# Rearranging a three-layer hybrid kernel: one image's linear attention beside the other's convolutions, and expert tiles between written attention steps

## The chip, the cores and the metric

The kernel runs on one core of a Trainium2 chip, as one program. The metric is the device time in microseconds (us). A core has five instruction streams: TensorE (PE, with its weight loads shown apart as PEld), VectorE (DVE), ScalarE (ACT), GpSimd (POOL) and SyncE (SP, which here only issues DMAs).

## The reference, cut to what matters

All arithmetic is fp32. The input is `x` of shape (2, 256, 56, 56): two images, 256 channels, 3136 pixels each.

```python
# layer 0, for each image
x = x + conv_ref(group_norm(x))
#   y = w_qkv1 @ x           1x1 convolution, 256 -> 768 channels
#   y = depthwise 3x3 of y   768 channels
#   q, k, v = y.reshape(B, H, W, 3, 8 heads, 32)     a raw reshape
#   heads 0-3: 7x7 neighbourhood attention; heads 4-7: the same, dilated by 2
#   o = w_proj @ heads
# layer 1 on t = the 2 x 3136 tokens of 256 features
t = t + attn(layernorm(t))
#   Q, K = elu(x Wq) + 1, elu(x Wk) + 1
#   KV = K^T v, summed over the image; msg = Q KV / (Q . sum K), then Wm, layernorm
#   h = relu([x, msg] W1) W2;  x + layernorm(h)
t = t + ffn(layernorm(t))
#   router: 8 experts, top 2 of softmax(x Wr + br)
#   each expert: layernorm, 256 -> 1024, gelu, 1024 -> 256; weighted sum of the two
```

The sum KV runs over a whole image, so no token's linear attention can start before the keys of all tokens of its image have been summed. The reshape mixes channels with pixels, so the attention of layer 0 can start on its first rows when the first channel groups are convolved.

## The kernel before, in words

The work is cut by image and by kind.

*Convolutions* (`convolutions`, L511). Each image has six groups of 128 output channels (`oc`), each in two halves of 28 rows: 12 blocks for an image. A block does the 1x1 convolution on TensorE (`py`, L531: four row groups) with a copy by ScalarE into a padded buffer (`ypad`, L537; there are two of them, one for each half). The 3x3 convolution is shared between the engines: eight of the 28 rows are nine matmuls with diagonal weights (`pc`, L552; GpSimd makes the diagonals at L520), the other 20 rows are one ScalarE and eight VectorE instructions (`yc`, L565 and L570). The block is stored to DRAM (`yd`).

*Neighbourhood attention* (`attend`, L736 and on). An image has 44 chunks: 28 of `band0` (not dilated) and 16 of `band1` (dilated). A chunk is: scores for four heads (L602, into `s_ps`, the only buffer of its kind, four PSUM banks), one exponential (L606), one multiplication by a table of biases and masks on VectorE (L607), then the values and the denominators (L612, into `po`, two banks), which VectorE adds to strips (L619). Queries and keys come by transposes of loaded rows (`prepare`, L685, through `s_ps` too). Finished strips are normalised (L629 to L639) and projected (`project`, L362 and L367), and the tokens go to DRAM (`td`).

*Linear attention* (`layer1`). For each pair of 128-token tiles, `keys` (L272) takes statistics, transposes, multiplies by Wk, applies elu and adds to `kx`. Then groups of four tiles go through four functions: `queries` (L1656 to L1670), `message` (L1696), `feed_forward` (L1726, L1742) and `route` (L1807 and on), which also scatters each token's row to its experts' lists in DRAM (`xs`, POOL queue, L161). Each function yields at its steps, and strings such as `"mqfpPPPPcufmuqfurfvrfvfv"` write out the order of these steps, one letter for each.

*Experts* (`Experts.run`). A tile is up to 256 rows of one expert: `fetch` loads the rows and 2.1 MB of weights, `turn` transposes, 32 matmul instructions make the hidden layer, with eight gelus (L1407, L1411), then 16 for each half of the rows make the output (L1425), and a scatter adds the rows to `y2`. A tile has eight steps. There are 48 full tiles and five half ones.

The order of the work: image 1's convolutions; from its third channel group on, image 1's attention beside them; image 2's convolutions beside the rest of that; then image 2's attention beside the keys of image 1 (`first_keys`); then all of the linear attention, the keys of image 2 within its first six steps. Four expert tiles (`NFI = 4`) lie between the last steps of the linear attention, the others come after it. In the first part a planner sets the order on each engine, from written priorities and estimated costs: each convolution step is followed by `PACE = 2` attention steps. From `layer1` on, TensorE's instructions run in the written order (`manual_schedule`); the other engines' orders are the planner's throughout. SP issues nearly all DMAs, in one queue that runs in order.

```python
for k, (b, blocks_done) in enumerate(convolutions()):       # front
    ...
    advance(PACE)
...
for k, _ in enumerate(first_keys(tokens, ps_e)):
    advance(3)
advance(10**6)
```

A pool's memory is used again by the next stage's pools. `NE1 = 32` is the number of token tiles after whose routing the first table of expert tiles is made.

Of the kernel before, what the change touches and what calls it, by code (L numbers as in the profile page):

```python
# [27 lines left out]
NA = -(-T // 128)  # L28
NH = 4
# [5 lines left out]
PACE = 2  # L35

# [16 lines left out]
NE1, NE2 = 32, 36  # L53
# [5 lines left out]
NFI = 4  # L59
# [60 lines left out]
def hybrid_kernel(ctx: ExitStack, tc: tile.TileContext, a: dict, out: bass.AP):  # L120
# [64 lines left out]
    class Tokens:  # L185


        def __init__(self, run):
            self.run = run
            self.rt, self.xa, self.kw = ExitStack(), ExitStack(), ExitStack()  # L190
            rt = self.rt.enter_context(tc.tile_pool(name=f"rt{run}", bufs=1, side="right"))

            self.t_ab = rt.tile([P, 1, C], F32, name="t_ab")
            self.xT_ab = rt.tile([P, 2, P], F32, name="xT_ab")

            self.up = rt.tile([P, NF], F32, name="up_t")
            self.cnt = rt.tile([P, E], F32, name="cnt")
            nc.gpsimd.memset(self.cnt, 0.0)

            xa = self.xa.enter_context(tc.tile_pool(name=f"ta{run}", bufs=1, side="right"))  # L200
            self.image = xa.tile([P, (NA + 1) * C], F32, name="t_a")
            self.t = [self.image[:, : (NA - 1) * C].rearrange("p (n c) -> p n c", c=C), None]

        def open(self):

            run = self.run
            xa = self.xa.enter_context(tc.tile_pool(name=f"xa{run}", bufs=1, side="right"))
            self.xT = [xa.tile([P, 2, (NA - 1) * P], F32, name="xT_a"), None]

            self.shared = self.image[:, (NA - 1) * C :].rearrange("p (n c) -> p n c", c=C)  # L210

            self.kxs = xa.tile([P, 2, C], F32, name="kxs0")
            self.kc = xa.tile([P, 2], F32, name="kc0")
            self.w_k = xa.tile([P, 2, C], F32, name="w_k")
            nc.gpsimd.dma_start(self.w_k, a["L1_attn_Wk"].rearrange("(k p) o -> p k o", p=P))
            self.b2 = xa.tile([P, C], F32, name="b2")
            nc.gpsimd.dma_start(self.b2, a["L1_attn_b2"].partition_broadcast(P))
            self.one = xa.tile([P, 1], F32, name="one")
            nc.vector.memset(self.one, 1.0)

        def at(self, n0, n):
# [3 lines left out]
            if n0 < NA:  # L225
                return self.t[0][:, n0 : n0 + n, :]
            k = (n0 - NA) % 4
            return self.t[1][(n0 - NA) // 4][:, k : k + n, :]

        def turned(self, n0, n):  # L230
# [4 lines left out]
            return self.xT[h][:, :, (n0 - h * NA) * P : (n0 - h * NA + n) * P]  # L235

        def load(self, n0, n, eng=nc.sync):
            self.loaded = eng.dma_start(
                self.at(n0, n), td[n0 * P : (n0 + n) * P, :].rearrange("(n p) c -> p n c", p=P)
            ).ins  # L240

    def elu1(wk, dst, src, tag, bufs):

        m = wk.tile([P, 512], F32, name=f"elu_{tag}", tag="tmp", bufs=bufs)[:, : src.shape[1]]
# [4 lines left out]
    def stats(sm, t, deviation=None):  # L249

        n = t.shape[1]
        st = sm.tile([P, max(n, 2), 6], F32, name="st")
        mv = sm.tile([P, 4, 2], F32, name="mv")
# [3 lines left out]
        return mv, rstd(sm, mv[:, :n, 1], 1.0, deviation)  # L257

    def rstd(sm, var, scale, deviation=None):
        n = var.shape[1]  # L260
        r = sm.tile([P, 2, 4], F32, name="rs")
        with tc.high_priority():
            nc.vector.tensor_scalar(r[:, 1, :n], var, scale, 1e-5, ALU.mult, ALU.add)  # L263
            newest[1] = nc.gpsimd.tensor_tensor(r[:, 0, :n], r[:, 1, :n], mhalf[:, :n], ALU.pow).ins  # L264
# [4 lines left out]
    def keys(tk, wk, sm, ps, bufs, kx, acc, n0, n):  # L269


        t = tk.at(n0, n)  # L272
        mv, rs = stats(sm, t, tk.up[:, n0 : n0 + n])
        xt = wk.tile([P, 2, C], F32, name="xt")
# [1825 lines left out]
```

## Time and profile before

| | |
|---|---|
| Median of three runs | 2033.22 us (2032.94 to 2037.04) |
| The profiled execution's own time | 2033.13 us |
| Its span, first to last instruction | 2031.3 us |
| Mean granted TensorE clock | 0.970 of full speed |
| Busy | PE 1871.8 us, PEld 1322.6, DVE 1034.5, ACT 617.3, POOL 654.5 |
| DMA | 264.65 MB, mean 130 GB/s |

The span is cut at these places, read from the timeline: at 437 us the last projection of image 1 has run and the first transposes of image 2's attention begin; from 757 us the queries of the linear attention run; at 840 us its steps are in rhythm; from 1162 us expert weights are loaded; at 1340 us the fifth expert tile starts, with nothing but experts after it. A busy share below the highest is not idle time by itself: the question in each stretch is which engine's work has to be waited for.

### The profile page before, as it was taken

What the parts mean: (1) busy time and instruction counts of PE and PEld (TensorE: products, weight loads), DVE (VectorE), ACT (ScalarE), POOL (GpSimd) and SP (SyncE); (2) the same over time, 40 slices, a digit from 0 to 9 for tenths busy, and PEclk for the clock granted to TensorE, in tenths of its full rate; (3) what the DMA queues carried; (4) which work ended last, traced back from release to release, by engine and by line L of the source; (5) the groups of instructions that cost most, each with busy time, mean ns of one, the idle gap of its engine ahead of it and who ended that gap; (6) DMA issues with size and microseconds to landing.
All of it is one profiled execution on the core that took longest, in us unless ns stands there. A gap on an engine that the chain in (4) does not pass through costs nothing.

```text
span 2031.3 us, 27712 instructions
## 1 busy us (share of the span) xinstructions
PE 1871.8 (92%) x10050; PEld 1322.6 (65%) x10050; DVE 1034.5 (51%) x2625; ACT 617.3 (30%) x1222; POOL 654.5 (32%) x776
## 2 busy tenths in 40 slices
PE   4999898999787888999999998999999999999995
PEld 2544454554445455665665657888888888888885
DVE  4987987877875666456555654442112211111221
ACT  1333334323232232333333323322222222222332
POOL 4522100122034234335434344523333332333321
PEclk9999899999889799999999999999999999999998
DMA  5542423344422125000111143577676767666995
GB/s 117 141 112 73 154 86 97 101 134 117 127 64 68 33 55 170 5 16 32 53 42 55 43 151 102 175 194 212 194 197 187 197 191 204 189 199 192 290 284 158
DMA packets 189976, 264.65 MB, mean 130 GB/s; under 512 B 26488, under 2 KB 149702, under 8 KB 189584
## 3 DMA queue, kind: packets, MB, share of 16 engines
q1 hardware_dynamic: 160912, 220.82, 35.4%
q0 software_dynamic: 20640, 29.76, 7.7%
q10 hardware_dynamic: 8272, 12.15, 1.7%
q8 instruction: 83, 1.36, 0.3%
q14 instruction: 69, 0.57, 0.1%
HBM read 196.39 MB, written 70.55 MB: 131 GB/s over the span
## 4 chain that ended last, share of the span: by engine, by line
PE 75%; DVE 10%; DMA 5%; POOL 3%; issue 3%; ACT 3%; SPq 0%; ACTq 0%; DVEq 0%; POOLq 0%
PE ph L1407 16%; PE py L1425 16%; PE p L1726 7%; PE pc L552 6%; PE py L531 5%; PE po L612 5%; PE py L1742 4%; PE s_ps L367 2%; PE kx L310 2%; DVE yc L570 2%; PE s_ps L602 2%; DMA y<-yt,idi 2%; PE kp L297 2%; DVE p L607 2%; PE pm L1696 2%
## 5 line engine op out<-in xcount | busy, mean ns | idle before, releaser
L1407 PE MATMUL ph<-xe,w1e 128*128 128x256 f32 (+1 forms) x1696 | 362.4, 371 | 3.2 <-DVE xe L1383 2.1
L1425 PE MATMUL py<-w2e,hT 128*128 128x256 f32 x1616 | 359.1, 379 | 0.0
L1411 ACT ACTIVATE hT<-ph,sv 128x256 f32<-128x256 f32 (+1 forms) x424 | 196.1, 463 | 498.9 <-PE ph L1407 496.1
L1407 PEld LDWEIGHTS ph<-xe,w1e 128*128 128x128 f32 x1696 | 310.2, 191 | 45.4 <-DVE xe L1383 3.0
L1425 PEld LDWEIGHTS py<-w2e,hT 128*128 128x128 f32 x1616 | 302.4, 190 | 39.0 <-issue 0.2
L570 DVE SCALAR_TENSOR_TENSOR yc<-ypad,w,yc 128x1120 f32<-128x1120 f32 x192 | 266.3, 1388 | 33.6 <-ACT yc L565 30.2
L161 POOL DMA_INDIRECT y<-yt,idi x101 | 160.7, 1591 | 218.9 <-DVE yt L1431 127.0
L552 PE MATMUL pc<-ypad,diag 128*128 128x448 f32 x432 | 177.5, 549 | 1.6 <-POOL acc L465 1.6
L1363 DVE CAST idi<-xr 128x2 int32<-128x2 f32 (+1 forms) x53 | 9.3, 176 | 317.2 <-DMA xr<-xs 306.5
L531 PE MATMUL py<-t_a,wq 128*128 128x448 f32 (+1 forms) x384 | 149.4, 525 | 11.4 <-DVE t_a L506 11.0
L1431 DVE SCALAR_TENSOR_TENSOR yt<-py,eq,yt 128x256 f32<-128x256 f32 x101 | 48.7, 483 | 207.6 <-PE py L1425 207.6
L606 ACT ACTIVATE p<-s_ps 112x952 f32<-112x952 f32 (+5 forms) x88 | 102.0, 1159 | 152.8 <-PE po L612 84.3
L264 POOL TENSOR_TENSOR rs<-rs,mhalf 128x2 f32<-128x2 f32 (+2 forms) x89 | 66.0, 749 | 239.9 <-DVE rs L263 188.1
L607 DVE TENSOR_TENSOR p<-p,tab 112x952 f32<-112x952 f32 (+5 forms) x88 | 125.1, 1425 | 32.1 <-ACT p L606 32.0
L520 POOL TENSOR_SCALAR diag<-ident,w 128x128 f32<-128x128 f32 x108 | 87.8, 831 | 142.8 <-PE pc L552 125.4
L552 PEld LDWEIGHTS pc<-ypad,diag 128*128 128x128 f32 x432 | 79.9, 192 | 70.4 <-issue 64.1
L531 PEld LDWEIGHTS py<-t_a,wq 128*128 128x128 f32 x384 | 70.2, 193 | 75.8 <-issue 58.8
L161 POOL DMA_INDIRECT xs<-row,si x98 | 99.1, 1011 | 63.3 <-DVE si L1862 30.1
L1389 POOL TENSOR_SCALAR yt<-b2e,eq 128x256 f32<-128x256 f32 x101 | 47.1, 473 | 224.2 <-DMA b2e<-in_L_ffn_b 217.8
L612 PE MATMUL po<-p,v 98*32 98x170 f32 (+5 forms) x960 | 77.8, 380 | 39.5 <-DVE p L607 16.7
L1742 PE MATMUL py<-fw,hTl 128*128 128x264 f32 x392 | 91.4, 389 | 3.3 <-DVE u L1749 3.3
L1726 PE MATMUL p<-m2T,fw 128*128 128x512 f32 (+2 forms) x224 | 94.1, 543 | 0.0
(388 smaller groups left out, 2522.7 us busy)
## 6 DMA issues: line engine op xcount, KB each, us to landing
w1e<-in_L_ffn_W SPq DMA_DIRECT2D x53, 1024.0 KB
w2e<-in_L_ffn_W SPq DMA_DIRECT2D x53, 1024.0 KB
yd<-yc SPq DMA_DIRECT2D x24, 784.0 KB
ld<-yd SPq DMA_DIRECT2D x28, 448.0 KB
xr<-xs SPq DMA_DIRECT2D x48, 260.0 KB
b2e<-in_L_ffn_b SPq DMA_DIRECT2D x53, 128.0 KB
yr<-y SPq DMA_DIRECT2D x11, 512.0 KB
td<-t_i SPq DMA_DIRECT2D x24, 224.0 KB
```

What stands on the lines that cost most here:

```text
L161: ins = nc.gpsimd.indirect_dma_start(out=dst[:, :], out_offset=bass.IndirectOffsetOnAxis(ap=index, axis=0), in_=src, in_offset=None, **kw,)
L531: nc.tensor.matmul(py[:, :n, :], wq1[:, ct, oc * P : (oc + 1) * P], x_sb[:, ct, (q0 + g0) * WW : (q0 + g0 + n) * WW], start=(ct == 0), sto ...
L552: nc.tensor.matmul(pc, diag[:, tap, :], ypad[:, dy : dy + 8, dx : dx + WW], start=(tap == 0), stop=(tap == 8),)
L570: nc.vector.scalar_tensor_tensor(yc[:, 8:, :], src, w, yc[:, 8:, :], ALU.mult, ALU.add)
L606: nc.scalar.activation(p[:nk, :, :n], s_ps[:nk, :, :n], AF.Exp)
L607: nc.vector.tensor_tensor(grid(p), grid(p), table[:nk], ALU.mult)
L612: nc.tensor.matmul(dst[hs] if w is None else den[hs], v[:nk, hs] if w is None else w[:nk, :], grid(p)[:, h, :, o : o + q.shape[2]], start= ...
L1407: nc.tensor.matmul(p1, x.w1[:, ct, j * P : (j + 1) * P], x.xe[:, ct, :], start=(ct == 0), stop=(ct == 1),)
L1411: nc.scalar.activation(hT[:, j, :], p1, AF.Gelu, bias=x.sv[:, 4 + j : 5 + j])
L1425: nc.tensor.matmul(py, hT[:, j, h * P : (h + 1) * P], x.w2[:, j, :], start=(j == 0), stop=(j == NJ - 1),)
L1726: nc.tensor.matmul(p1[:, :w], fw1[:, k, oc * P : (oc + 1) * P], rhs, start=(k == 0), stop=(k == 3))
L1742: nc.tensor.matmul(py[:, : C + E], hT[:, kk, c0 : c0 + P], fw2[:, kk, :], start=(kk == 0), stop=(kk == 3),)
```

## The change

- **Classes.** `front` is taken apart into a class `Convolutions`, a class `Attention` (one object for each image) and `first_image`.
- **First image.** `first_image` runs the convolutions of image 1 as before, and image 1's attention beside them with two steps for each convolution step, three once image 2's convolutions have begun. When that attention has ended, `conv.share`'s pools are closed, and `run` (the rest of the convolutions) is handed on. By the counts of the two generators this happens in the fourth of image 2's 12 blocks; before, with two steps throughout, it happened in the sixth.
- **Convolutions alone.** The eight blocks that are left use no diagonals and no `pc` matmuls: all 28 rows are done by ScalarE (first tap) and VectorE (eight taps), in two strips of 14 rows. Each of these blocks has nine steps. They have one PSUM bank.
- **Linear attention by image.** `linear(ph, tk, half)` makes pools, loads and functions for one image, so all weights are loaded and prepared twice (`feed`, `router`). The first image's keys and six groups (24 tiles) run in written TensorE order, with a convolution step for each `k` in the strings and two for each key pair. Its summed keys (`sums[0]`) are stashed in DRAM for the tile that both images share. All loads are on SP; before, most weights were on POOL's queue. `keys` loses the code for a shared tile: each image takes its half of tile 24 itself.
- **Fills.** The 16 stores of constant rows into `y2` and `xs` (4.3 MB) were issued at the second step of the linear attention; now they are issued behind the first image's last scatter and ahead of the second image's attention.
- **Second image's attention.** It runs alone in written TensorE order. Scores of a chunk come before the values of the chunk before it (`pending`); transposes and projections are single pieces (`side`) that stand at the places between them; at places that have no such piece, an expert tile's step is issued: after all scores, and after values when the step's number is a multiple of four. They have two PSUM banks together. The first 12 places make the table of expert tiles.
- **Then** the second image's keys and groups, with expert steps at `e` and two for each key pair. `NFI` is 13 in place of 4, `NE1` 24 in place of 32, and `hT`, the hidden layer's tile, has one buffer in place of two.

The core of the diff, with the parts that were only moved left out:

```diff
-NE1, NE2 = 32, 36
+NE1, NE2 = 24, 36
...
-NFI = 4
+NFI = 13
+LEAD = 12
...
+        def alone(self):
+            self.dp, self.banks = None, self.banks[:1]
...
                 for hf in range(2):
+                    shared = SHARE if self.dp is not None else 0
...
+                    strips = [(SHARE, HH // 2)] if shared else [(0, HH // 4), (HH // 4, HH // 2)]
                     for tap in range(9):
...
+                        for y0, y1 in strips:
...
-                        if tap % 3 == 2:
+                        if tap % 3 == 2 if shared else tap % 2 == 0:
                             yield b, oc
...
+            def side():
+                if turning:
+                    turning.popleft()[1]()
+                elif aside and aside[0][0] <= count[0]:
+                    aside.popleft()[1]()
+                else:
+                    return False
+                return True
+            def step(first, rest, then, n=1):
...
+                first()
+                yield "aside" if side() else "scores"
+                if pending:
+                    for f in pending.popleft():
+                        f()
+                pending.append((rest, then))
+                count[0] += 1
+                yield "aside" if side() else "values"
...
+            for _ in range(PACE + b):
+                if need is not None and need <= done:
+                    need = next(steps, None)
+            if need is None:
+                break
+        ctx.close()
+        return run
...
-                hT = self.w.tile([P, NJ, ST], F32, name="hT")[:, :, : nh * P]
+                hT = self.w.tile([P, NJ, ST], F32, name="hT", bufs=1)[:, :, : nh * P]
...
+            ln = linear(ph, tk, 0, behind)
+            with tc.manual_schedule(engines={mybir.EngineType.PE}):
+                for i, _ in enumerate(ln.keys()):
+                    if i == 5:
+                        ln.feed()
+                    if i % 3 != 1:
+                        fill()
+                fill(2)
+                merging = ln.close()
+                prepared = ln.router()
+                parts = (
+                    "qkwkxkwkxkwkxkqk", "mkqkmkqk", "mkqkfkmqfkfkfkffk",
+                    "mqfkfkPPPPmqfrfkrffk", "mqfkpPPPPfkmqfrfrkff", "mqfkpPPPPfkmqfrfrkff",
+                    "mkfkpPPPPfkmfrfrkff", "fkpPPPPkfkfrfkrfkf", "kpPPPPkrkkrkk", "kpPPPPk",
+                )
...
+                ln.keep()
+                nc.sync.dma_start(y2[N : N + ST, :], a["c_fill"][0, :, 0:C])
+                for i in range(NDUM):
+                    rows_i = slice(E * RG + i * ST, E * RG + (i + 1) * ST)
+                    nc.sync.dma_start(xs[rows_i, :], a["c_fill"][E + i])
...
+                att = Attention(ph, 1, "l t b k v p r x ac", bank)
+                with tc.manual_schedule(engines={mybir.EngineType.PE}):
+                    for i, what in enumerate(att.run()):
+                        if i < LEAD:
+                            next(table, None)
+                        elif what == "scores" or what == "values" and i % 4 == 0:
+                            next(tiles, None)
...
+                for i, _ in enumerate(ln.keys()):
+                    if i == 5:
+                        ln.feed()
+                    if i % 3 != 1:
+                        next(tiles, None)
...
+                parts = (
+                    "qewexewexewexeqe", "meqemeqe", "meqefemqfefefeff",
+                    "mqfpPPPPfmqfrfrff", "mqfpPPPPfmqfrfrff", "mqfpPPPPfmqfrfrff",
+                    "mqfpcfmfqrfPPfPrPfe", "mqfpfmfqePePrePfePref", "mfefpefmeferePPfePerPe",
+                    "fefeepefeferePfePere", "eeeeperPePer", "eeeepP",
+                )
```

## The prediction

> **What bounds the kernel now.** I read the page's engine totals and slices first, then busy times by stretch, then groups by line, then what TensorE waited for in the weakest stretch.
>
> ```profile
> PE 1871.8 (92%) x10050; PEld 1322.6 (65%) x10050; DVE 1034.5 (51%) x2625; ACT 617.3 (30%) x1222; POOL 654.5 (32%) x776
> PE   4999898999787888999999998999999999999995
> DVE  4987987877875666456555654442112211111221
> PEclk9999899999889799999999999999999999999998
> ```
>
> TensorE bounds the whole, but its bad slices are the eleventh to sixteenth, where no engine is full and the clock is low. The stretches (columns: length; busy PE, PEld, DVE, ACT, POOL with counts; clock; DMA):
>
> ```profile
> 0.00:255.00 255.00, 213.93 (x1100) 110.30 (x1104) 200.86 (x228) 75.44 (x118) 88.40 (x114) 0.97 0.45 119
> 255.00:437.00 182.00, 172.19 (x1280) 93.04 (x1269) 153.45 (x171) 61.02 (x79) 27.07 (x39) 0.99 0.34 97
> 437.00:550.00 113.00, 102.43 (x636) 54.04 (x635) 86.96 (x116) 35.94 (x56) 15.35 (x18) 0.95 0.46 122
> 550.00:757.00 207.00, 164.98 (x1439) 100.41 (x1438) 127.17 (x240) 63.60 (x82) 67.78 (x83) 0.88 0.23 65
> 757.00:840.00 83.00, 72.54 (x318) 51.11 (x317) 49.76 (x137) 24.99 (x57) 39.55 (x59) 0.96 0.34 104
> 840.00:1162.00 322.00, 315.13 (x1240) 199.78 (x1239) 189.26 (x776) 109.60 (x290) 129.90 (x148) 1.00 0.12 39
> 1162.00:1340.00 178.00, 163.15 (x768) 125.68 (x767) 88.19 (x490) 57.56 (x136) 80.14 (x93) 0.96 0.46 141
> ```
>
> From the first convolutions to 437, VectorE is the fuller partner (153 of 182 us, 84%). From 550 to 757 (image 2's attention, image 1's keys) PE is 80% busy at clock 0.88 and VectorE 61%: latency, not work. From 840 PE is 98% busy. After 1340 there are only experts. So 437 to 840 has idle time to fill, and the end has work that could fill it.
>
> ```profile
> L1407 PE MATMUL ph<-xe,w1e 128*128 128x256 f32 (+1 forms) x1696 | 362.4, 371 | 3.2 <-DVE xe L1383 2.1
> L1425 PE MATMUL py<-w2e,hT 128*128 128x256 f32 x1616 | 359.1, 379 | 0.0
> L570 DVE SCALAR_TENSOR_TENSOR yc<-ypad,w,yc 128x1120 f32<-128x1120 f32 x192 | 266.3, 1388 | 33.6 <-ACT yc L565 30.2
> L552 PE MATMUL pc<-ypad,diag 128*128 128x448 f32 x432 | 177.5, 549 | 1.6 <-POOL acc L465 1.6
> L606 ACT ACTIVATE p<-s_ps 112x952 f32<-112x952 f32 (+5 forms) x88 | 102.0, 1159 | 152.8 <-PE po L612 84.3
> L607 DVE TENSOR_TENSOR p<-p,tab 112x952 f32<-112x952 f32 (+5 forms) x88 | 125.1, 1425 | 32.1 <-ACT p L606 32.0
> L1411 ACT ACT_TABLE_LOAD x5 | 6.4, 1283 | 8.3 <-PE ph L1407 8.3
> PE po L612 <- DVE p L607: 8.4, 8, 3.8
> ```
>
> One expert tile costs (362.4 + 359.1) / 50.5 = 14.3 us of PE (48 full, 5 half). The last row, from the waits of 437 to 757, shows PE held for a chunk's exponential and table product.
>
> **The change, part by part**, against the profiled span of 2031.3 us.
>
> *Stage 1, to the end of image 1's attention: 414 us.* Before, 437. The third attention step per convolution step ends the same attention two blocks sooner. Two blocks take 16 x 1.388 = 22 us of VectorE, the fuller engine, and 2 x (177.5 + 149.4)/24 = 27 us of PE: I take 23.
>
> *Stage 2, image 1's linear attention beside eight blocks: 360 us.* Removed: 8 x 177.5/24 = 59 us of PE and four sets of diagonals on POOL (36 x 0.83 = 30 us, hidden). Added: VectorE does 28 rows in 16 instructions of 784 elements instead of 8 of 1120. No such form is in the trace; scaling 1388 ns by length gives 0.97 us, unscaled it would be 1.39. I take 0.97, as instructions of 512 elements take 0.68. So 8 x 16 x 0.97 = 124 us of VectorE (to 178). The rest of VectorE: 13 key pairs at about 3.6 us (statistics, norms, copy, elu) = 47; a group, from 840 to 1162, (189.3 - 8 x 3.6)/7.75 = 20.7, six are 124; preparations about 13. Sum 308. PE: routing matmuls (L1853) come 42 us apart while two key pairs are in each step and 33 us apart after, so 33 a group and some 4 a pair; blocks 6.2 (149.4/24): 52 + 196 + 50 + 8 = 306. Both are equally full, in orders fixed beforehand. At VectorE's 84 to 89% of the convolution stretches (start-up of 30 us left out): 346 to 367, I take 356, plus 4 at the start. ScalarE's copies into `ypad` wait for VectorE's taps of two blocks earlier; queued behind them are elu, relu and squares, for which PE waits.
>
> *The hand-over, in stage 3: 20 us.* The fills, hidden before, now wait for the last scatters of image 1 (8 at 1.0 us behind the last routing). On SP, the image-2 loads can queue behind them: 4.3 MB at the 173 to 190 GB/s that loading stretches show is 23 us. If SP is ordered around them it costs 8; if all in series, 40. I take 20, nearest to the fills alone.
>
> *Stage 3, image 2's attention with 4.4 expert tiles: 225 us with the hand-over.* 114 places, 37 of them with an expert step: two start, 35 make 4.4 tiles. VectorE: half of lines 607, 619 and the smaller ones, 135 us, and 14 for the tiles: 149. PE: half the attention rows, 178 (overlapping ones counted twice, so 110 to 178), plus 63: 173 to 241. ScalarE: exponentials 51, copies 15, gelus 16, and table switches. Each hidden-layer step stands between two exponentials: 19 steps, 38 loads of 1.28 us = 49. Sum 131. None is full; 205 is the middle of PE's bounds, against 207 for 550 to 757, which had the keys' 50 us of PE in place of 63 for tiles, and much of the attention done before it.
>
> The Trainium skill ("ScalarE: Activation LUTs", What ACT_TABLE_LOAD costs) speaks against interleaving: it gives about 2.66 us for a switch, with a drain, and advises batching. The trace has the gelu start 1.29 us after the load does. By the page ScalarE would hold 183 us in this stage, still under 205.
>
> *Stage 4, image 2's keys and groups with 8.6 tiles: 416 us.* PE: 52 + 6.25 x 32.5 + 8 + 8.6 x 14.3 = 386. The shares before were 98% (840 to 1162) and 92% (1162 to 1340, with tiles): at 95%, 406. Plus 10: the preparation stands at the sixth key step and needs weights that are loaded behind 3 MB of tokens.
>
> *Stage 5, experts alone: 563 us.* 2031.3 - 1340 = 691.3, less nine tiles at 14.3. One buffer for `hT` costs nothing: PE's order already puts a tile's last output matmul before the next tile's first hidden one. If the cover failed, a gelu of 0.46 us per tile would show, 16 us.
>
> Sum: 414 + 360 + 225 + 416 + 563 = 1978; the run takes 1.8 more than its span: **1980**, 53 under. The profiled run is 0.1 below the median, so no correction.
>
> **The rivals.**
>
> *All seams close*: expert steps fill every gap, the fills hide. Stage 2 at VectorE's 92% is 335, stage 3 is 190, stage 4 is 400: 1904. For: from 840 on, written order gave PE 98%. Against: never with convolutions beside it.
>
> *Slower: VectorE holds up stage 2.* Its 308 us are as long as PE's, so every late tap stops ScalarE, then PE, then VectorE's own next inputs. At the 70% between 550 to 757 (61%) and 437 to 550 (77%) the stage takes 440 and the total is 2060. It decides above 413 us, a share below 75%. Unscaled 784-element taps (1.39) would do it as well: 362 / 0.87 = 416. For: 33.6 us of idle before L570. Against: the earlier convolution stretches kept 84%.
>
> *The hand-over eats it*: fills, weights and row loads in one SP queue stop attention again and again; stage 3 takes 275 and the total is 2030, no change. For: SP alone now issues all. Against: DMA was 23% busy from 550 to 757.
>
> **How the numbers follow.** Forecast 0.52 (its own range 1935 to 2022), all seams close 0.25, VectorE 0.18, hand-over 0.05. Within 0.2%, 4 us, is about what this kernel's runs can tell from no change. Faster: 0.52 + 0.25 less 0.01 of the forecast's tail, 0.76; same 0.04; slower 0.20. The range reaches down to 1910, near the second case, and up to 2045 into the third.
>
> **What would show it.** Right: `pc` (L552's successor) has 288 instructions, not 432; PE busy near 1820; some 60 table loads; from the last expert-only tile count, 35 full tiles in about 500 us; VectorE above 80% beside the late convolutions; a PE gap of 10 to 30 us before image 2's first transposes. Wrong: stage 2 over 400 us, or stage 3 over 260 with PE waiting for row loads, or the expert tiles more than 14.5 us apart.

## The result and the profile after

The changed kernel takes 2175.26 us (median of four runs, 2169.75 to 2191.33) against 2033.39 us for the kernel before on the same chip. The ratio is 1.0708, 95% interval 1.0659 to 1.0756: 142 us slower, where 53 us faster had been forecast. The profiled execution is the longest of the four, 2191.33 us with a span of 2189.5 us, so the stage lengths below hold about 16 us more than a median run. Part of that is in stage 1, where its clock was 0.93 and which took 439 us; the kernels below that leave this stage as it is show 428 to 439.

From the page of the changed kernel, the engine totals and the slices (40 slices of the span, in tenths):

```profile
PE 1878.1 (86%) x9960; PEld 1331.2 (61%) x9960; DVE 1080.8 (49%) x2712; ACT 682.3 (31%) x1275; POOL 631.3 (29%) x729
PE   4999897657889991589977988999969999999996
DVE  4979986476867664256645332554452122121121
PEclk9999898778899995599988999999979999999998
```

Before, the weak slices were the eleventh to the sixteenth. Now weak ones are spread from the seventh to the thirtieth, and one is nearly empty (the sixteenth: PE at 1, the clock at 5). PE busy did not fall by the 59 us counted for the removed `pc` matmuls; it rose by 6. The matmuls that stayed took longer: the mean granted clock fell from 0.970 to 0.928, and a hidden-layer matmul between attention steps took 414 ns on average, where 371 ns is the average before. The 54 that came on top, most of them for the weights' second preparation, are few.

```profile
L1514 PE MATMUL x<-xe,w1e 128*128 128x256 f32 x152 | 41.1, 414 | 2.2 <-ACT hT L1518 1.2 <-DVE kT L181 0.7 <-DVE yt L1538 0.2
```

Busy time by stretch, changed kernel (columns: stretch; length; busy PE, PEld, DVE, ACT, POOL with counts; clock; DMA share; GB/s):

```profile
0.00:439.00 439.00, 364.53 (x2270) 194.09 (x2271) 323.85 (x374) 126.27 (x179) 94.25 (x124) 0.93 0.37 101
446.00:566.00 120.00, 86.40 (x321) 63.09 (x320) 91.03 (x177) 29.70 (x51) 68.20 (x75) 0.84 0.16 50
566.00:701.00 135.00, 121.83 (x395) 71.17 (x396) 94.51 (x215) 48.14 (x117) 14.05 (x15) 0.91 0.08 29
701.00:845.00 144.00, 118.02 (x463) 70.99 (x462) 101.31 (x384) 38.79 (x99) 64.07 (x61) 0.92 0.22 72
845.00:884.00 39.00, 8.42 (x39) 5.99 (x42) 6.57 (x40) 2.84 (x7) 12.94 (x17) 0.50 0.53 152
884.00:1144.00 260.00, 217.85 (x1988) 139.16 (x1984) 137.19 (x233) 121.72 (x145) 29.97 (x37) 0.88 0.51 135
1151.00:1279.00 128.00, 109.56 (x494) 90.41 (x495) 50.94 (x164) 46.66 (x72) 70.28 (x92) 0.93 0.38 110
1279.00:1419.00 140.00, 129.40 (x508) 85.11 (x508) 56.43 (x190) 53.32 (x122) 22.98 (x27) 1.00 0.17 49
1419.00:1613.00 194.00, 166.89 (x761) 122.58 (x760) 95.34 (x505) 54.85 (x142) 83.84 (x90) 0.93 0.28 82
1613.00:2189.00 576.00, 553.77 (x2730) 488.03 (x2730) 118.29 (x411) 160.03 (x344) 168.44 (x186) 0.98 0.73 213
```

Row by row: image 1's attention ends; image 1's keys; its ramp, from the first queries to the first routing; the rest of its groups; the hand-over; image 2's attention with tiles; image 2's keys; its ramp; the rest with tiles; experts alone. Two seams of 7 us, ahead of each key stretch, are left out. The two key stretches take 120 and 128 us. In the kernel before there was no such stretch at all. From 446 to 845 VectorE is 72% busy (286.9 of 399 us), not over 80%, and TensorE 82% (326 us).

What TensorE waited for from 446 to 845 (the first two lines) and from 845 to 900 (the third), and SP's own queue from 845 to 900 (the fourth); columns: us in total, times, longest:

```profile
PE kx L301 <- DVE ks L238: 32.5, 13, 11.1
PE pp L1953 <- DVE chosen L1945: 19.2, 1, 19.2
PE x L705 <- DMA ld<-yd: 34.5, 6, 24.4
SPq L2073 <- DMA xs<-row,si: 14.2, 1, 14.2
```

The key phase waits for its own elu, once per pair (`ks`). The end of image 1's half waits once for 19 us, behind convolution taps that stand between the small steps of the last routing on VectorE. Then the fills wait on SP for the scatters to land, the row loads of image 2's attention stand behind them, and TensorE waits for those (34.5 us).

Each stage against the prediction, in us of the profiled execution:

| Stage | Predicted | Measured | Over |
|---|---|---|---|
| 1, to the end of image 1's attention | 414 | 439 | 25 |
| 2, image 1's linear attention | 360 | 406 | 46 |
| Hand-over and 3, image 2's attention | 225 | 299 | 74 |
| 4, image 2's keys and groups | 416 | 469 | 53 |
| 5, experts alone | 563 | 576 | 13 |

The overruns add to 211 us, the distance from the predicted sum of 1978 to the span. No one stage carries it.

### The profile page after: what moved, and what is told of

The parts are those of the page before. It is cut to its first block, busy times and chain, and to the rows that moved or that the text cites. A ratio compares the mean times of both kernels' runs of the same rounds, so it can differ in the third digit from the quotient of the medians.

```text
span 2189.5 us, 27684 instructions
## 1 busy us (share of the span) xinstructions
PE 1878.1 (86%) x9960; PEld 1331.2 (61%) x9960; DVE 1080.8 (49%) x2712; ACT 682.3 (31%) x1275; POOL 631.3 (29%) x729
## 4 chain that ended last, share of the span: by engine, by line
PE 63%; DVE 15%; DMA 8%; issue 4%; ACT 4%; POOL 4%; SPq 1%; DVEq 0%; POOLq 0%; ACTq 0%
PE ph L1514 13%; PE py L1532 12%; PE p L1826 7%; DVE yc L545 5%; PE py L506 4%; PE po L614 4%; PE pc L525 4%; PE kx L301 2%; DMA y<-yt,idi 2%; PE s_ps L600 2%; PE py L1842 2%; PE pq L1756 2%; PE pm L1796 2%; PE s_ps L341 1%; POOL rs L255 1%
## 5 line engine op out<-in xcount | busy, mean ns | idle before, releaser
L1514 PE MATMUL ph<-xe,w1e 128*128 128x256 f32 (+1 forms) x1544 | 334.9, 373 | 8.4 <-DMA w1e<-in_L_ffn_W 4.4
L1532 PE MATMUL py<-w2e,hT 128*128 128x256 f32 x1488 | 337.0, 382 | 0.0
L545 DVE SCALAR_TENSOR_TENSOR yc<-ypad,w,yc 128x1120 f32<-128x1120 f32 (+1 forms) x256 | 315.2, 1237 | 26.9 <-ACT yc L540 23.6
L1514 PEld LDWEIGHTS ph<-xe,w1e 128*128 128x128 f32 x1544 | 283.4, 193 | 48.7 <-issue 5.5
L1518 ACT ACTIVATE hT<-ph,sv 128x256 f32<-128x256 f32 (+1 forms) x386 | 177.5, 462 | 428.4 <-PE ph L1514 425.8
L506 PE MATMUL py<-x_sb,wq 128*128 128x448 f32 (+1 forms) x384 | 151.6, 529 | 14.4 <-DVE x_sb L477 13.7
L255 POOL TENSOR_TENSOR rs<-rs,mhalf 128x2 f32<-128x2 f32 (+3 forms) x90 | 70.0, 785 | 311.3 <-DVE rs L254 210.1
L506 PEld LDWEIGHTS py<-x_sb,wq 128*128 128x128 f32 x384 | 72.2, 197 | 76.4 <-issue 55.6
L525 PE MATMUL pc<-ypad,diag 128*128 128x448 f32 x288 | 116.2, 545 | 0.2 <-ACT ypad L512 0.2
L301 PE MATMUL kx<-xt,ks 128*128 128x256 f32 (+1 forms) x200 | 59.5, 448 | 42.3 <-DVE ks L238 42.3
L1826 PE MATMUL p<-xT,fw 128*128 128x512 f32 (+1 forms) x208 | 94.1, 576 | 0.0
```

The costliest lines, as they stand in the source:

```text
L301: nc.tensor.matmul(kx[:, hg, :], ks[:, k, hg * P : (hg + 1) * P], xt[:, k, :], start=(first and k == 0 and hg == 0), stop=(last and k == n ...
L506: nc.tensor.matmul(py[:, :n, :], self.wq1[:, ct, oc * P : (oc + 1) * P], self.x_sb[:, ct, (q0 + g0) * WW : (q0 + g0 + n) * WW], start=(ct ...
L525: nc.tensor.matmul(pc, diag[:, tap, :], ypad[:, dy : dy + SHARE, dx : dx + WW], start=(tap == 0), stop=(tap == 8),)
L545: nc.vector.scalar_tensor_tensor(yc[:, y0:y1, :], src, w, yc[:, y0:y1, :], ALU.mult, ALU.add)
L1514: nc.tensor.matmul(p1, x.w1[:, ct, j * P : (j + 1) * P], x.xe[:, ct, :], start=(ct == 0), stop=(ct == 1),)
L1518: nc.scalar.activation(hT[:, j, :], p1, AF.Gelu, bias=x.sv[:, 4 + j : 5 + j])
```

## The experiments

After the result, the theory was this. Cutting the linear attention into two halves gives each image a key phase with nothing to hide it, and a ramp and a run-out of its own; the seams come on top. The rivals: VectorE holds up stage 2; expert tiles and table loads hold up stage 3; image 1's attention is slowed by the new ratio of steps. Every ratio below is to the kernel before, measured beside it, and the changed kernel's own, 1.0708, is the mark. Where an interval meets its interval (1.0659 to 1.0756), the time alone decides nothing and the stage lengths do. For image 2's attention, from its first scores to its last projection, kernels that left it as it was show 252 to 261 us in their profiles; the changed kernel's own, 260, is among the longest.

### The cover of the keys, taken away from the kernel before

The first edit of the kernel before runs image 1's keys when image 2's attention has ended:

```diff
-        for k, _ in enumerate(first_keys(tokens, ps_e)):
-            advance(3)
         advance(10**6)
+        with tc.issue_after(anchors["tokens"]):
+            for k, _ in enumerate(first_keys(tokens, ps_e)):
+                pass
```

> The kernel before, with one edit: image 1's keys run after image 2's attention has ended, not beside it. Theory (an image's keys fill about 50 us of TensorE and take 105 to 128 us when nothing else is there, so the cover was worth the difference): image 2's attention ends 20 to 30 us sooner, the keys then take 105 to 130 us alone, the total rises by 80 to 100 us, ratio 1.04 to 1.05. Rival (keys cost their 50 us of TensorE wherever they lie, and the loss is elsewhere): the attention gets shorter by about what the keys take, total 0 to 30 us above before, ratio 1.00 to 1.015.

Measured: 2131.43 us against 2032.75, ratio 1.0499 (1.0467 to 1.0531). Its stretches of attention alone and of keys alone, and TensorE's longest wait in the latter:

```profile
536.00:739.00 203.00, 132.93 (x1283) 76.20 (x1284) 105.03 (x147) 48.92 (x56) 9.15 (x13) 0.82 0.32 90
742.00:855.00 113.00, 74.28 (x258) 53.10 (x258) 38.47 (x122) 19.40 (x33) 64.80 (x94) 0.80 0.10 31
PE kx L310 <- DVE ks L247: 28.8, 12, 6.5
```

The last projection of image 2 comes 42 us sooner, at 739 in place of 781 (20 to 30 had been expected), and the keys then take 113 us. The first routing is at 997 in place of 916. The profiled execution took 2114.84 us, 17 under the median, so its stretches show some 82 of the 99 us. Here the keys are ordered by the planner, not by hand, and the same wait for `ks` shows: 28.8 us, against 32.5 in the changed kernel. So the long key phase is not the fault of the written order.

The second edit of the kernel before runs image 2's twelve key pairs ahead of the groups, in the three-deep order that the changed kernel uses:

```diff
+                live = {}
+                for i in range(14):
+                    for k in (2, 1, 0):
+                        j = i - k
...
+                        if 0 <= j < 12:
+                            next(live[j])
...
-                    if s < 6:
-                        for k in range(2):
-                            on["uv"[k]] = keys(tk, wk, sm, ps_a, 4, kx, acc, groups[7 + s][0] + 2 * k, 2)
```

> The kernel before, with one edit: image 2's twelve key pairs run by themselves ahead of the first group, in the three-deep order that the changed kernel has, not inside the first six groups' steps. Theory (a key phase by itself is latency): the six steps fall from 42 to about 33 us each (-54 us), the key phase takes 105 to 125 us, total +45 to +70 us, ratio 1.022 to 1.034. Rival (the keys cost the same at either place): 54 us less and 50 to 60 us more, ratio 0.997 to 1.007.

Measured: 2078.87 us, ratio 1.0237 (1.0201 to 1.0272). Its key phase, and the ramp behind it:

```profile
773.00:869.00 96.00, 62.06 (x252) 49.64 (x252) 39.09 (x107) 17.29 (x30) 59.03 (x79) 0.88 0.15 48
869.00:976.00 107.00, 97.42 (x349) 59.03 (x348) 46.92 (x160) 36.74 (x98) 12.21 (x16) 0.97 0.03 10
```

The key phase takes 96 us with TensorE 65% busy; 105 to 125 had been expected. The wait for `ks` is 28.5 us there. Inside the groups' steps it had been 0.3 us (the first line is of this kernel from 773 to 869, the second of the kernel before from 757 to 916):

```profile
PE kx L310 <- DVE ks L247: 28.5, 12, 3.1
PE kx L310 <- DVE ks L247: 0.3, 1, 0.3
```

There the same pairs had made the ramp 22 us longer (129 us from 787 to 916, against 107) and the two steps between the next routings 9 us each, 40 us in all, not the 54 of the expectation. The two edits cost 99 and 46 us. Both totals lie in the ranges that the theory gave, and outside the rival's. That their sum, 145, is as much as the whole loss of the changed kernel (142) is in part chance: there, convolution and expert steps stand beside the keys, and other terms come on top.

### The third attention step

Added to the kernel before by itself:

```diff
-            advance(PACE)
+            advance(PACE + b)
```

> The kernel before, with one edit: three attention steps are issued for each convolution step once image 2's convolutions have begun. Theory (image 1's attention is paced by its own chain, not by the ratio): it ends at 430 to 440 us as before, at 437, and the total stays within 10 us, ratio 0.995 to 1.005. Rival (the prediction's step): it ends near 414 us, two blocks of convolution are left for later, and the total changes by 10 to 25 us in either direction.

Measured: ratio 0.9987 (0.9965 to 1.0009), 2028.36 us. Image 1's last projection is at 432 us, 435 before. The step that the prediction counted at 23 us is worth nothing there. Taken out of the changed kernel:

```diff
-            for _ in range(PACE + b):
+            for _ in range(PACE):
```

> Two attention steps for each convolution step throughout, so that image 1's attention has six of image 2's blocks beside it and six are left for the linear attention, not eight. Theory (the attention's pace is set by its own chain of scores, exponential, table and values, not by the ratio of steps; the third step only takes its cover away): attention still ends near 437 us, two blocks of work are gone from the next stage, and the time falls by 20 to 35 us. Rival (the ratio sets the pace): attention ends 20 us later and the total moves less than 10 us.

Measured: 2153.14 us, ratio 1.0613 (1.0584 to 1.0642), an interval clear of the changed kernel's: some 20 us less, the lower end of what the theory gave. Its first two stages:

```profile
0.00:432.00 432.00, 375.30 (x2339) 197.90 (x2340) 343.35 (x390) 133.47 (x191) 98.14 (x133) 0.98 0.38 106
438.00:814.00 376.00, 313.82 (x1142) 198.42 (x1142) 257.92 (x743) 109.19 (x254) 139.15 (x151) 0.90 0.15 50
```

The attention ends no later with fewer steps per convolution step (432 us; with three steps 428 to 439), and more convolution is done by then (VectorE 343 us against 324), so stage 2 falls from 399 to 376 us. Between two and three steps the ratio does not pace stage 1. That the attention's own chain does is the theory's reason, which no run isolates; with one step, below, the end does move, to 489. The third step only pushed convolution out of a place where it was hidden.

### Is VectorE the bound of stage 2?

The eight late blocks with the split of the earlier ones (eight rows on TensorE, with diagonals); to make room, `elu`'s scratch tiles have three buffers in place of four, and the diagonals one:

```diff
-            self.dp = None
+            self.dp = pool("p1d", 1, side="right")
...
-            self.dp, self.banks = None, self.banks[:1]
+            self.banks = self.banks[:1]
```

> The eight blocks beside the linear attention keep their diagonal matmuls for 8 of 28 rows: TensorE gets 54 us more work, VectorE 35 us less (8 x 4.4) in half as many instructions. One scratch tile has three buffers in place of four to make room. Theory (VectorE's share and the order of its taps set this stage): the stage stays within 10 us of 400 us or gets shorter, and the total moves by -20 to +10. Rival (TensorE sets it): the stage and the total grow by 35 to 55 us.

Measured: 2225.49 us, ratio 1.096 (1.0934 to 1.0985). Its stage 2:

```profile
442.00:882.00 440.00, 376.69 (x1320) 224.95 (x1320) 246.66 (x710) 116.60 (x266) 153.93 (x178) 0.94 0.13 46
```

VectorE's work falls by 40 us (to 56% of the stage), TensorE's grows by 50, and the stage is 41 us longer than the 399, as the rival said. VectorE's busy time did not hold it up. The edit does more than move rows, though: a block with diagonals has four steps, one without has nine, so with the same strings seven of the eight blocks now lie in the key phase, which takes 190 us in place of 120, while the rest of the stage takes 250 in place of 279. So the some 50 us by which the total grows are the price of the whole edit, its denser order and fewer buffers included, and not of the eight rows alone.

One attention step, not three, while image 2's convolutions run, so that little convolution is left beside the linear attention:

```diff
-            for _ in range(PACE + b):
+            for _ in range(PACE - b):
```

> One attention step for each convolution step once image 2's convolutions run, so that nearly all of them (all but the last block) lie beside image 1's attention with TensorE's share, and image 1's linear attention runs almost alone. Theory (VectorE's taps stand in the linear attention's chains and cost it about 100 us): the linear stage falls from 400 us (440 to 841) to 270 to 300, the first stage grows from 437 to 510 to 530, and the total falls by 20 to 50 us. Rival (the linear attention of one image has the same waits alone): its stage stays above 340 us and the total grows.

Measured: ratio 1.0735 (1.0715 to 1.0756), not distinguishable from the changed kernel. Image 1's attention ends at 489 and its linear attention, now nearly alone, still takes 339 us, where the theory gave 270 to 300:

```profile
504.00:843.00 339.00, 280.71 (x1047) 182.09 (x1047) 165.22 (x646) 86.41 (x218) 128.08 (x149) 0.90 0.11 35
```

That is 105 us of keys and 234 us for six groups, 39 us each, where a group in rhythm took 33; 114 of the 234 lie before the first routing. With VectorE half idle, the half still takes 339 us: these waits are its own. And the convolutions cost about the same in either place: stage 1 grew by 50 us, the linear attention fell by 60, and the seam between them grew by 8.

### The hand-over

The fills issued behind the key phase, before any routing, so that they no longer wait for scatters:

```diff
+                nc.sync.dma_start(y2[N : N + ST, :], a["c_fill"][0, :, 0:C])
+                for i in range(NDUM):
...
                 fill(2)
                 merging = ln.close()
```

> The 16 stores of constant rows are issued when the first image's keys are summed, as early as before the change, and not behind its last scatter. Theory (the hand-over between the images' stages is a chain: last taps, routing, scatters, stores, row loads): TensorE's 24.4 us wait for the second image's rows shrinks to about 10, and the time falls by 10 to 20 us. Rival (the stores are hidden and the row loads wait for something else): no change within 1%.

Measured: 2165.5 us, ratio 1.0661 (1.061 to 1.0712). The gap from the last routing matmul to image 2's first scores falls from 39 to 29 us, and TensorE's longest wait for rows from 24.4 to 11.0. The same, with a convolution step after every key step, so that no taps stand beside the last routing:

```diff
-                    if i % 3 != 1:
-                        fill()
+                    fill()
```

> The constant rows are stored early, and each of the 39 key steps of image 1 has a convolution step behind it, not two of three, so that the last block's taps are done some 60 us before the last routing. Theory (the hand-over is a chain of the last taps, the last routing between them, scatters, stores and loads): TensorE's 19 us wait for `chosen` goes too, and the time from the last feed-forward matmul to image 2's first scores shrinks from about 70 us to about 45; the total falls by 20 to 35 us. Rival (VectorE bounds the stage, so that taps moved forward only make the keys later): the total moves less than 12 us.

Measured: 2163.34 us, ratio 1.0653 (1.063 to 1.0676). The gap is 30 us, and TensorE's wait for `chosen` falls from 19.2 to 9.9 us, but image 1's key phase grows from 120 to 134, with VectorE 88% busy in it. A total some 11 us under the changed kernel's is the rival's figure, not the theory's 20 to 35. The fills are about 10 us of the hand-over. The rest, scatters, row loads and transposes one after the other, these edits did not shorten.

### Expert tiles between the steps

No tiles in image 2's attention (they are left to the experts' own stage):

```diff
-                        elif what == "scores" or what == "values" and i % 4 == 0:
-                            next(tiles, None)
```

> No expert step between the second image's attention steps; the 4.4 tiles run densely at the end of the second image's stage instead. Theory (attention in written order leaves TensorE little idle time, and the rest is small matmuls, so that a tile there costs its full 14.3 us or more): the attention stage falls from about 251 us (893 to 1144) by 55 to 75, the end grows by 63, and the total is within 15 us of the changed kernel's. Rival (the tiles fill waits): the attention stage falls by under 30 us and the total grows by over 35.

Measured: 2185.98 us, ratio 1.0773 (1.0738 to 1.0808). The attention by itself:

```profile
877.00:1089.00 212.00, 157.46 (x1689) 91.27 (x1688) 125.58 (x194) 63.10 (x74) 11.43 (x16) 0.80 0.44 112
```

212 us, against some 255 with 4.4 tiles, whose own price is 63 us. So about 43 us of the 63 were paid in the attention and 20 were hidden, which is between the theory (55 to 75 paid) and the rival (under 30). TensorE is busy for 157 of the 212 us: the attention alone is not held by TensorE's work. Relu in place of gelu in the interleaved tiles, which needs no table of its own (the output differs by that function):

```diff
-                    nc.scalar.activation(hT[:, j, :], p1, AF.Gelu, bias=x.sv[:, 4 + j : 5 + j])
+                    nc.scalar.activation(
+                        hT[:, j, :], p1, AF.Relu if nh == 2 and t < NFI else AF.Gelu, bias=x.sv[:, 4 + j : 5 + j]
+                    )
```

> The 13 full tiles that run between other work use a relu in place of the gelu, so that ScalarE needs no other table for them; part of the computation is changed, the number of instructions is the same but for the table loads (60 in the changed kernel, under 10 here). Theory (seams and lost cover, not tables): the total falls by less than 15 us. Rival (each switch delays the exponentials or the gelus that TensorE waits for): 51 loads of 1.28 us, and the total falls by 40 to 65 us.

Measured: 2158.85 us, ratio 1.0652 (1.062 to 1.0685); attention 246 us, image 2's keys 121 in place of 128. The 33 table loads are about 10 us of the attention. The 7 us of the key phase are not shown to be theirs: without tiles in the attention (the run before this one) it also takes 121 us, with 18 loads in it, where the changed kernel has 13.

Two tiles more, at every key step and three places of the ramp:

```diff
-NFI = 13
+NFI = 15
...
-                    if i % 3 != 1:
-                        next(tiles, None)
+                    next(tiles, None)
...
-                    "qewexewexewexeqe", "meqemeqe", "meqefemqfefefeff",
+                    "qeewexeewexeewexeqe", "meqemeqe", "meqefemqfefefeff",
...
-                    if i > 2:
+                    for _ in range(3 if i > 2 else 0):
                         chunk(work)
```

> The changed kernel with 15 expert tiles between the steps in place of 13: one expert step after every key step of image 2 (39 places in place of 26) and three more in the ramp behind them; the later tiles' table is made in fewer steps so that it is ready. Theory (TensorE's empty places in key phase and ramp can be filled for nothing): these stages stay within 10 us of 128 and 139, the experts alone shrink by two tiles (28 us), ratio 1.055 to 1.062 to before in place of 1.071. Rival (the stages are full in the written order, or bound by the tiles' own transposes and loads): they grow by the 23 to 28 us that the tiles take, and the ratio stays at 1.068 to 1.074.

Measured: 2180.11 us, ratio 1.0722 (1.067 to 1.0773): the rival. Its key phase, and its ramp:

```profile
1132.60:1278.30 145.70, 127.88 (x607) 109.73 (x608) 56.26 (x179) 59.17 (x89) 78.86 (x100) 0.96 0.43 127
1278.30:1425.50 147.20, 136.81 (x528) 89.42 (x526) 57.16 (x192) 55.83 (x127) 23.91 (x28) 0.99 0.18 53
```

A tile has eight steps, so one step is 14.3 / 8 = 1.8 us. The two stretches take 146 and 147 us, 293 together, where the changed kernel's took 268: 16 steps cost 25 us, 1.6 each, nearly the full price. The experts alone fell by 20 us, not 28: between two of their first tiles lie 22 us in place of 14.3, with a 6 us wait for rows (`xr`) that the changed kernel does not have there. The same two tiles put in the last two strings instead, where tiles are up to 42 us apart:

```diff
-NFI = 13
+NFI = 15
...
-                    "fefeepefeferePfePere", "eeeeperPePer", "eeeepP",
+                    "fefeepefeferePfePere", "eeeeeepeereePeePeeer", "eeeeeepeeeeeeP",
...
-                    if i > 2:
+                    for _ in range(3 if i > 2 else 0):
                         chunk(work)
```

> The changed kernel with two more expert tiles, placed in the last two strings of image 2's groups, where the last routings end and 42 us lie between the hidden layers of two neighbouring tiles in place of 14.3. Theory (a tile that stands where no other work is left fills idle time, unlike one that stands between key steps): the experts alone shrink by 28 us, the drain grows by 5 to 15 us, ratio 1.059 to 1.065 in place of 1.071. Rival (each written expert step is charged in full wherever it stands, as between the key steps): the drain grows by 28 us, ratio 1.069 to 1.073.

Measured: 2180.4 us, ratio 1.0738 (1.071 to 1.0767): no gain, as the rival said. The stretch from the first routing to the experts is 216 us in place of 194; 16 steps cost 22 us, 1.4 each, nearer the rival's 28 than the theory's 5 to 15. The experts alone fell by 23 us, with the same wait for rows.

### The order inside the key phase, and all repairs together

Convolution and expert steps placed behind the key products and the transposes, where the elu is awaited, in both key phases:

```diff
-                    if i % 3 != 1:
+                    if i % 3 != 0:
```

> In both key phases the work between the key steps stands behind the key matmuls and the transposes, not behind the sums and the transposes, so that about 4 us of TensorE work and not 2.2 lies between a pair's key matmuls and its sum, which need relu, exponential, addition (2 us) and, beside tiles, table loads. Theory (the written order leaves too little between a pair's steps): the waits of kx for ks (32 us and 10 us) fall by half or more, and the total falls by 15 to 30 us. Rival (VectorE's order is to blame): they stay and the total moves under 8 us.

Measured: 2163.78 us, ratio 1.0644 (1.0623 to 1.0665). The wait of `kx` for `ks` falls from 32.5 to 27.6 us in image 1's phase and from 9.8 to under 1 in image 2's; the phases shrink by about 5 us each. The total falls by some 13 us, between the theory (15 to 30) and the rival (under 8): the wait goes in image 2's phase and mostly stays in image 1's. Then two steps throughout, fills and taps early, and this order for image 2's tiles, in one kernel:

> The changed kernel with the small gains so far in one: two attention steps for each convolution step throughout (-19 us by itself), fills ahead of the routings and a convolution step after every key step (-12), expert steps behind both of the later key pieces (-12, of which 5 are in image 2's keys). Theory (what is left is the loss of the cover that image 1's keys and image 2's keys had, which two edits of the kernel before priced at 98 and 46 us): the gains add to 30 to 40 us, the time is 2130 to 2145 us, ratio 1.047 to 1.056, still far above before. Rival (one chain of small waits, each of which holds up the next, so that together they give more than their sum): below 2110 us, ratio under 1.038.

Measured: 2145.57 us, ratio 1.0561 (1.0539 to 1.0584), at the upper edge of what the theory gave. The repairs add to less than their sum: two steps alone had given 1.0613. 115 us remain. No run pointed to a version that beats the kernel before.

## Why the prediction was wrong

**The step that failed** is the busy share that turned TensorE's and VectorE's sums into stage lengths, in stages 2 and 4. I took 84 to 89% and 95% from stretches in full rhythm (the convolutions, and 840 to 1340), and applied them to stages that begin with a key phase and a ramp. Measured were 72% of VectorE in stage 2, and 82 and 88% of TensorE in stages 2 and 4. Keys entered as 52 us of matmuls in each half. Alone they are a chain, one wait for elu per pair, and took 96 us (image 2's twelve pairs ahead of the groups), 105 (image 1's beside almost nothing), 113 (image 1's after the attention); with other steps written between, 120 and 128. In the kernel before, one image's keys lay beside attention and the other's inside the groups' steps, and this chain was mostly covered. I priced what the keys got as cover in the new place, and never what they lost in the old one. The two edits of the kernel before show that price there: 99 and 46 us. The chain was in sight: in the kernel before, the longest of TensorE's waits from 437 to 757, two lines above the one that I quoted, is

```profile
PE kx L310 <- DVE ks L247: 15.2, 9, 3.8
```

The sums were off too: TensorE had 326 us in stage 2 and 406 in stage 4, where I had 306 and 386. That is some 20 us of each overrun (46 and 53); the share is the rest. These two stages hold 99 of the 211 us. The largest single overrun, stage 3's 74, is another step, below.

**Stage 1** was wrong in its one argument. I counted the blocks no longer done before the attention's end and took their time off. Going from two steps to three does not move that end (435 and 432 us in the kernel before; in the changed one 432 with two, 428 to 439 with three). The 23 us were imaginary, and the third step cost about 20 in stage 2.

**Stage 2.** The instruction counts held: `pc` has 288 instructions, and a tap of 784 elements took 1.08 us on average where I had scaled to 0.97.

```profile
L525 PE MATMUL pc<-ypad,diag 128*128 128x448 f32 x288 | 116.2, 545 | 0.2 <-ACT ypad L512 0.2
L545 DVE SCALAR_TENSOR_TENSOR yc<-ypad,w,yc 128x784 f32<-128x784 f32 x128 | 136.9, 1079 | 8.0 <-ACT yc L540 7.1
L1518 ACT ACT_TABLE_LOAD x30 | 38.5, 1283 | 21.5 <-PE ph L1514 21.0
```

That is 13 us more of VectorE than the 124 counted, and it does not decide the stage: VectorE's whole sum came to 287 us, not 308, and TensorE's to 326, so the two were not equally full. My slower rival named the right sign and a share below 75% (it was 72%), but its cause is not what the runs show: with 40 us less on VectorE the stage grew, and with almost no taps beside it the linear attention still took 339 us.

**The hand-over** was inside its bounds of 8 to 40, at the upper end: 39 us. I had weighed the fills alone, and they were 10. The run-out before it, which waits 19 us for VectorE, was not in the sum.

**Stage 3.** The step that failed here is the 205 us, the middle of TensorE's bounds with the tiles in it. The attention alone takes 212 us with TensorE 74% busy, so its length is not a sum of TensorE's work, and what the keys left was not room for the tiles. With them it took 260; the tiles hid a third of themselves. The table loads came as counted: `L1518`, the hidden layer's own, shows 1283 ns each, 60 loads in all. They cost the stage about 10 us. The Trainium skill ("ScalarE: Activation LUTs", What ACT_TABLE_LOAD costs) gives 1283 ns for the load and some 1380 ns more for a drain, 2.66 us for a switch. The load agrees. The drain does not show: 55 of the 60 loads start 17 to 19 ns after the end of ScalarE's instruction ahead of them, and behind 50 the next one starts after 11 or 12 ns.

**Stage 4** repeats stage 2's error: 128 us of keys where 52 + 46 at 95% is 103, and 334 us for ramp and groups where I had some 313 with the preparation.

**Stage 5** ran at 14.3 us a tile as predicted. The 13 us are a misreading: at 1340 us the fifth tile of the kernel before was already 13 us old (tiles start at 1327 and 1344), so only eight tiles, not nine, came off.

Two signs named in advance as right failed, VectorE above 80% and PE busy near 1820, and two named as wrong came: stage 2 over 400 us, and stage 3 over 260 with its start waiting for row loads. I had put 0.20 on slower, nearly all of it on VectorE, which was not the cause.

What stays open: the terms do not add up to a proof. The lost cover (145), the third step (about 20), the hand-over (some 30) and the table loads (about 10) make over 200 us, less some 50 for the removed `pc` rows. That is near the 142, but these come from different kernels: the 145 are for keys with nothing beside them, which is not so in the changed kernel, and the 50 are from an edit that also moved the convolution. That the keys lose when they stand by themselves is shown; how much of the 142 that is, is not. Neither the second ramp nor the second preparation of the weights was measured by itself.

## What to carry to other kernels

Before work is moved, measure what hid it in its old place: a phase that must finish a sum before its users start is a chain of waits, and cost about twice its matmul time here (96 to 113 us for some 52) when nothing stood beside it. Take the busy share for a new stage from a stretch of the same kind, a start from a start and a key phase from a key phase, not from steady rhythm. Work that is written between the steps of a latency-bound phase is not free; here half to nine tenths of its price were charged, wherever it stood.

## What the runs showed of the hardware that I had not expected

A phase with gaps pays twice. In the hand-over TensorE was busy for 8.4 of 39 us and the granted clock was 0.50; image 2's attention without tiles ran at 0.80, keys alone at 0.80 to 0.88, groups in rhythm at 1.00. In such phases the matmuls are longer themselves (414 ns against 371 in image 2's attention with tiles, at a clock of 0.88), and PE "busy" rose although 144 matmuls of 545 ns were gone. The Trainium skill ("TensorE: Matmul & The Clock Gate", What's actually happening) has the clock at half after an idle window of some 3.4 us and at full after as long a busy one. The 0.50 of the hand-over agrees; the length of the window was not measured here.

The busy share of TensorE does not say how much can still be fitted in. Image 2's key phase showed 110 of 128 us busy with 26 expert steps. That is 1.2 us each above the 96 us of twelve key pairs alone, or 0.9 above the 105 of image 1's thirteen; the next 16, there and in the ramp, cost 1.6 each of their 1.8.
